# Carrying the scan state into the first source element on ScalarE instead of through the scan's initial value

## The chip, the cores and the metric

The kernel runs on one core of one Trainium2 chip. The metric is device time in microseconds (us) from the first to the last instruction of the program, as each run reports it; less is better. A profile is one further execution of the same program, recorded instruction by instruction. TensorE does matrix products, VectorE and GpSimd do elementwise work, ScalarE does activations and copies, and SyncE issues the transfers. In the profile's lines they are called PE, DVE, POOL, ACT and SP.

## The reference, cut to what matters

The reference is a network of four stages on an image batch of shape 4 x 96 x 64 x 64. Its first stage (`L0`) holds a selective scan, and that scan is most of the time. For each of 4 images and 4 directions (rows forward, columns forward, and both backward) the sequence has 4096 positions; there are 192 channels, and each channel has 16 states:

```python
def step(hst, inp):
    dt_t, x_t, B_t, C_t = inp
    dA = jnp.exp(dt_t[..., None] * A[None])
    dBx = dt_t[..., None] * B_t[:, :, None, :] * x_t[..., None]
    hst = hst * dA + dBx
    y_t = jnp.einsum('bkdn,bkn->bkd', hst, C_t)
    return (hst, y_t)
h0 = jnp.zeros((b, K, D_INNER, D_STATE), t.dtype)
```

So the state `hst` is a first-order recurrence along the sequence, multiplied by a decay `dA` and fed by a source `dBx` at each position. The rest of the network (a convolution, layer norms and an MLP, a second scan with one state per channel, an FFT stage, linear attention, two quantized MLPs) is work for each image that comes before or after its scan.

## The kernel before, in words

**Units.** A scan of one image and one direction is cut along the sequence into 4 chunks of 1024 positions (`CH`). The 192 x 16 = 3072 pairs of channel and state fill the 128 partitions 24 times. A *unit* is one such filling of one chunk: a tile of 128 x 1024. There are 4 images x 4 directions x 4 chunks x 24 = 1536 units, numbered `i`; unit `i` of chunk `s` (`s` = 0 to 3) continues unit `i - 24` of chunk `s - 1`. `steps[g]` gives image `b`, direction `k`, chunk number `s` and place `c`; for `k >= 2` the sequence runs backward, and the scan reads its tiles in reverse.

**What a unit does**, and on which engine:

- `sources()`, GpSimd: `w = u * bb`, the source (line `w<-u,bb` in the profile). `w` has 6 buffers.
- `decays()`, ScalarE: `h = Exp(dt * negA)`, the decay, into PSUM (`h<-dt,negA`). `h` has 2 buffers, so this `Exp` of unit `i` needs unit `i - 2` to be through.
- `recurs()`, VectorE: the scan, `h = scan(h, w)` (`h<-h,state,w` or `h<-h,w`), and then `w = h * cc` (`w<-h,cc`). In every 12th unit the scan writes `w` instead and GpSimd multiplies by `cc` (`side()`).
- `gathers()`, TensorE: four products with `sel4` sum `w` over the states into PSUM `py` (`py<-w,sel`), two units at a time.
- `decays()` again, two units later, ScalarE: where another chunk follows, a copy of the last column of `h` into `state[:, n]` (`state<-h`, 128 x 1).

In the kernel before, a scan in a chunk with `s > 0` has that column of `state` as its initial value, an operand of one number for each partition; in a chunk with `s = 0` its initial value is the constant 0.

**Order.** [...]each engine runs its instructions in the order in which they were issued. That order is made while the program is built by a planner, the class `Work`. The kernel is written as generators ("threads") that `yield on(engine, events...)` before each piece of work; the planner holds an estimated clock for each engine, picks the piece that can start first, and adds the estimated cost. `decays()` is its *lead* thread: `choose()` skips other ScalarE work that would hold up the lead. `latest()` tells by when the lead of a unit is due, out of the pace of the scans, with the constants `UNIT` (us a unit), `MARGIN` and `YIELD`; `AGE` lets ScalarE work that has waited long go ahead of the lead. All the work outside the scans (`others()`: fronts of later images, and for finished images `tail`, `l1`, `l2` and `back`) is background: it goes into the gaps beside the units. What is left of it when the last scan is over runs alone. For the last image `tail()` first normalizes four blocks of columns (`gate`, with its lines `yc<-...`), and then runs eight groups of 512 columns through a projection, a norm and an MLP (`group`, lines `x<-...`, `hn<-...`, `s<-...`), each ending in `stat<-x`; `l1` begins when all eight statistics are there.

Every VectorE and GpSimd instruction is recorded with line 254 (a helper), an activation with line 242, a ScalarE copy with line 231, a product with line 227. They are told apart by their tiles.

Of the kernel before, what the change touches and what calls it, by code (L numbers as in the profile page):

```python
# [12 lines left out]
AF = mybir.ActivationFunctionType  # L13
ALU = mybir.AluOpType
# [3 lines left out]
B, C, HH, WW = 4, 96, 64, 64  # L18
# [3 lines left out]
CH = 1024  # L22
# [3 lines left out]
UNITS = 24  # L26

LN_EXP = "natural_log_exp_and_others"
# [17 lines left out]
def size(x):  # L46
    return x.free_size() if hasattr(x, "free_size") else x[:].free_size()


def on(engine, *events, banks=0, took=0.7, table=None, unit=None):  # L50


    return engine, events, banks, took, table, unit
# [9 lines left out]
class Work:  # L63
# [2 lines left out]
    GAP = 0.25  # L66
    LEAD = 1.0
    PATIENCE = 0.0
    UNIT, MARGIN, YIELD, AGE = 3.6, 0.5, 0.8, 0

    def __init__(self):
        self.at = dict(pe=0.0, act=0.0, dve=0.0, pool=0.0, sp=0.0)
# [31 lines left out]
    def post(self, *key, stored=False):  # L104
        self.events[key] = self.me.stored if stored else self.me.end
# [111 lines left out]
def tile_hybrid(ctx: ExitStack, tc: tile.TileContext, I: dict, out: bass.AP):  # L217
    nc = tc.nc
    wk_ = Work()
# [9 lines left out]
    def copy(o, i, **kw):  # L229
        wk_.spend("act", 0.15 + size(o) * 0.87e-3)  # L230
        return nc.scalar.copy(o, i, **kw)  # L231

    def act(o, i, func, **kw):

        want = TABLES.get(func, func if func in OTHER else None)
        if want is not None and want != wk_.table:
            wk_.spend("act", 1.28)
            if func in TABLES:
                nc.scalar.preload_act_table_set(want)
            wk_.table = want  # L240
        wk_.spend("act", 0.2 + size(o) * 0.87e-3)
        return nc.scalar.activation(o, i, func, **kw)  # L242
# [25 lines left out]
    ve, po_ = Side(nc.vector, "dve", on_vector), Side(nc.gpsimd, "pool", on_pool)  # L268
# [27 lines left out]
    def open_banks(n, name="bk"):  # L296
        st, (p,) = pools(psum(name, 1))
        names = [f"{name}{k}" for k in range(n)]
        wk_.open(p, names)
        st.callback(wk_.close, names)  # L300
        return st
# [26 lines left out]
    def setup():  # L328
        yield on("act")
        act(negA, V("A", n=96), AF.Exp)  # L330
        act(l1A, V("l1A", n=2), AF.Exp)
        yield on("dve")
        ve.tensor_scalar_mul(negA, negA, -1.0)
        ve.tensor_scalar_mul(l1A, l1A, -1.0)
        for j in range(3):
            ve.reduce_sum(dsum[:, j : j + 1], V("Ds", j=4 * j, n=4), axis=mybir.AxisListType.X)
            ve.tensor_scalar(diagD[:, j], eye128, dsum[:, j : j + 1], None, ALU.mult)
        ve.reduce_sum(dsum[0:C, 3:4], V("l1D", C, n=2), axis=mybir.AxisListType.X)
        ve.tensor_scalar(centd, cent, dsum[0:C, 3:4], None, ALU.mult)
        for lay in (2, 3):  # L340
            yield from ffn_weights(lay)
# [986 lines left out]
    def rest(b):  # L1328
# [16 lines left out]
    steps = [  # L1345
        (b, k, s, NCH - 1 - s if k >= 2 else s) for b in range(B) for k in (0, 1, 3, 2) for s in range(NCH)
    ]
    NS_ = len(steps)
    NU = UNITS * NS_
    WB, DB, RB, SIDE = 6, 3, 5, 12  # L1350
    made, weights = {}, {}
    live = dict(h={}, w={}, state={}, Y=None, py=None)
    fg = {}

    def place(i):
        n = i % UNITS
        j, r = divmod(n, 8)
        q, p = divmod(r, 2)
        return i // UNITS, j, q, p, (2 * j + p) * 4 + q
# [104 lines left out]
    def decays():  # L1464
        for i in range(NU + 2):
            if i >= 2:
                yield on("act", ("scan" if (i - 2) % SIDE == SIDE - 1 else "C", i - 2), *([("dt", 6 * place(i)[0] + 2 * place(i)[1] + place(i)[3])] if i < NU else []), took=1.3, table=LN_EXP, unit=min(i, NU - 1))
                g, j, q, p, n = place(i - 2)
                b, k, s, c = steps[g]
                h = live["h"].pop(i - 2)  # L1470
                if s < NCH - 1:
                    last = 0 if k >= 2 else CH - 1
                    copy(live["state"][b, k][:, n : n + 1], h[:, last : last + 1])
                    post("st", i - 2)
            else:
                g, j, q, p, n = place(i)
                yield on("act", ("dt", 6 * g + 2 * j + p), took=1.3, table=LN_EXP, unit=i)
            if i < NU:
                g, j, q, p, n = place(i)
                k = steps[g][1]  # L1480
                h = live["h"][i] = fg["h"].tile([128, CH], F32, tag="h", name="h")
                act(h, made[g]["dt", 2 * j + p], AF.Exp, scale=negA[:, k * 24 + n : k * 24 + n + 1])
                post("h", i)

    def sources():
# [10 lines left out]
    def recurs():  # L1496
        for i in range(NU):
            g, j, q, p, n = place(i)
            b, k, s, c = steps[g]
            need = [("h", i), ("src", i), ("cc", 4 * g + q)]  # L1500
            if s:
                need.append(("st", i - UNITS))
            yield on("dve", *need)
            wk_.pace = i, max(wk_.me.start, wk_.at["dve"])
            if i % UNITS == 0 and s == 0:
                live["state"][b, k] = fg["ck"].tile([128, 24], F32, tag="state", name="state")
            h, w, state = live["h"][i], live["w"][i], live["state"][b, k]
            first = 0.0 if s == 0 else state[:, n : n + 1]
            o = w if i % SIDE == SIDE - 1 else h
            if k >= 2:  # L1510
                ve.tensor_tensor_scan(o[:, ::-1], h[:, ::-1], w[:, ::-1], first, ALU.mult, ALU.add)
            else:
                ve.tensor_tensor_scan(o, h, w, first, ALU.mult, ALU.add)
            if o is w:
                post("scan", i)
                live["h"][i] = o
                continue
            yield on("dve")
            ve.tensor_mul(w, h, made[g]["cc", q])
            post("C", i)  # L1520
# [99 lines left out]
    with tc.manual_schedule():  # L1620
        stb = open_banks(3, "bm")
        st = open_banks(5, "bs")
        mode["wide"] = True
        first = wk_.add(setup()), wk_.add(front(0))
# [10 lines left out]
        wk_.events["go",] = wk_.events["inproj", 0]  # L1635
        ts = [wk_.add(f(), 0) for f in (preludes, collects, convolved, gathers, side, sources)]
        wk_.lead = wk_.add(decays(), 0)
        ts += [wk_.lead, wk_.add(recurs(), 2), wk_.add(loads_du(), 0), wk_.add(loads_bc(), 0)]
        others_ = wk_.add(others())
        wk_.run(lambda: all(t.done for t in ts))  # L1640
# [181 lines left out]
```

## Time and profile before

| what | value |
|---|---|
| three runs, median (lowest to highest) | 6655.88 us (6654.35 to 6673.25) |
| the profiled execution's own time | 6648.81 us |
| its span, first to last instruction | 6647.0 us |
| mean granted TensorE clock | 0.871 |
| VectorE busy | 5807.2 us (87%) |
| GpSimd busy | 4740.5 us (71%) |
| ScalarE busy | 4308.0 us (65%) |
| TensorE busy (matmul) | 5289.4 us (80%) |

By stage, from the table of busy times in windows of the span:

| window, us | what runs | VectorE | ScalarE | GpSimd |
|---|---|---|---|---|
| 0 to 160 | front of image 0, first units | 39% | 42% | 27% |
| 700 to 6000 | units, with background beside them | 90 to 96% | 58 to 79% | 78 to 82% |
| 6085 to 6647 | rest of the last image, no units | 36% | 53% | 0% |

A group line of the profile reads: line, engine, operation, written tile `<-` read tiles, shapes, `x`count, then busy us and the mean ns of one, then how long the engine was idle just before these instructions and what ended that idle time. A line of the waits reads: who waited `<-` for whom, us in total, times, longest. A line of the timeline reads: start us, duration us, engine, line, operation, tiles.

### The profile page before, as it was taken

The numbers are of one execution on the slowest core, as the hardware profiler recorded it, in microseconds if no ns is written. First come the engines' busy times: TensorE is split into PE (matmuls) and PEld (weight loads), VectorE is DVE, ScalarE is ACT, GpSimd is POOL, SyncE is SP. The second block draws the span as 40 slices with busy tenths as digits, with TensorE's granted clock in tenths as the row PEclk, the third lists the DMA queues.
The fourth block names the chain that finished last, engine by engine and source line by source line (L and its number), as shares of the span: only waits on it lengthen the run. The fifth ranks groups of instructions, "written<-read, shape, count | busy, mean of one in ns | idle before, by whom it ended". The sixth has DMA issues, their size and how long they took to land. (4 is left out here: it accounts for less than half of the span.)

```text
span 6647.0 us, 55955 instructions
## 1 busy us (share of the span) xinstructions
PE 5289.4 (80%) x15752; PEld 1653.6 (25%) x15752; DVE 5807.2 (87%) x3872; ACT 4308.0 (65%) x6520; POOL 4740.5 (71%) x2148
## 2 busy tenths in 40 slices
PE   7678888977867888767777888877777888877788
PEld 2122221222211332212211232212211232212273
DVE  4898989899989999999989999999989999996613
ACT  4565756666766557876666567887666567885636
POOL 2778787787798787787698687787698687883000
PEclk8689999978879999888778999889778999888778
DMA  5656566565555685555555585555565586552451
GB/s 146 191 169 193 164 187 189 166 196 182 174 181 163 214 283 174 168 188 177 161 183 163 186 295 186 165 185 186 164 183 163 182 294 186 169 178 76 154 158 34
DMA packets 532384, 1189.24 MB, mean 179 GB/s; under 512 B 90158, under 2 KB 163451, under 8 KB 532060
## 3 DMA queue, kind: packets, MB, share of 16 engines
q1 hardware_dynamic: 532072, 1185.66, 57.0%
q8 instruction: 125, 2.05, 0.1%
q14 instruction: 187, 1.53, 0.1%
HBM read 937.80 MB, written 247.63 MB: 178 GB/s over the span
## 5 line engine op out<-in xcount | busy, mean ns | idle before, releaser
L254 POOL TENSOR_TENSOR w<-u,bb 128x1024 f32<-128x1024 f32 x1536 | 3607.6, 2374 | 907.0 <-PE py L227 785.3
L254 DVE TENSOR_TENSOR_SCAN h<-h,state,w 128x1024 f32<-128x1024 f32 x1056 | 2480.8, 2349 | 177.5 <-ACT h L242 89.2
L227 PE MATMUL py<-w,sel 128*32 128x512 f32 x6144 | 1847.9, 930 | 511.3 <-DVE w L254 381.7
L242 ACT ACTIVATE h<-dt,negA 128x1024 f32<-128x1024 f32 x1536 | 1727.7, 1125 | 428.5 <-DVE w L254 304.1
L254 DVE TENSOR_TENSOR w<-h,cc 128x1024 f32<-128x1024 f32 x1408 | 1721.8, 1223 | 109.5 <-DVE h L254 3.2
L254 DVE TENSOR_TENSOR_SCAN h<-h,w 128x1024 f32<-128x1024 f32 x352 | 805.5, 2288 | 112.7 <-POOL w L254 60.0
L231 ACT COPY state<-h 128x1 f32<-128x1 f32 x1056 | 166.2, 157 | 762.7 <-DVE w L254 761.1
L227 PEld LDWEIGHTS py<-w,sel 128*32 128x32 f32 x6144 | 188.0, 114 | 1595.7 <-DVE w L254 962.2
L254 POOL TENSOR_TENSOR w<-w,cc 128x1024 f32<-128x1024 f32 x128 | 301.9, 2358 | 165.6 <-ACT state L231 92.9
L227 PE MATMUL bm<-xp,dg 128*128 128x512 f32 x792 | 372.1, 616 | 0.9 <-ACT dtu L242 0.9
L227 PE MATMUL bm<-xi,xw 128*128 128x512 f32 x384 | 225.3, 733 | 99.8 <-DMA xi<-xi_d 84.6
L254 POOL TENSOR_TENSOR dtu<-dtu 128x1536 f32<-128x1536 f32 x64 | 221.3, 3458 | 84.7 <-ACT dtu L242 49.7
L242 ACT ACTIVATE dtu<-bm 128x512 f32<-128x512 f32 x384 | 209.0, 599 | 65.5 <-PE bm L227 62.8
L227 PE MATMUL bm<-xd,dtw 64*128 64x512 f32 x384 | 218.8, 654 | 21.8 <-ACT xd L242 9.9
L254 DVE TENSOR_TENSOR_SCAN w<-h,state,w 128x1024 f32<-128x1024 f32 x96 | 224.8, 2342 | 2.9 <-ACT h L242 2.7
L254 POOL TENSOR_TENSOR dtu<-dtu,xi 128x1536 f32<-128x1536 f32 x64 | 220.9, 3452 | 3.9
L227 PEld LDWEIGHTS bm<-xp,dg 128*128 128x128 f32 x792 | 148.5, 195 | 281.8 <-issue 263.0
L227 PE MATMUL bm<-big,dg 96*96 96x512 f32 x432 | 208.6, 625 | 10.8 <-ACT u L242 7.6
L227 PE MATMUL py<-Y,eye 128*128 128x512 f32 x288 | 166.2, 660 | 42.6 <-ACT Y L231 39.8
L242 ACT ACTIVATE bm<-bm,eps 96x512 f32<-96x512 f32 (+1 forms) x210 | 135.7, 646 | 64.7 <-PE bm L227 64.4
L242 ACT ACT_TABLE_LOAD x119 | 152.7, 1283 | 20.7 <-PE bm L227 18.7
L227 PE MATMUL bm<-x,cent 96*96 96x512 f32 x278 | 148.9, 628 | 19.6 <-DMA x<-in_x 5.5
(317 smaller groups left out, 6994.6 us busy)
## 6 DMA issues: line engine op xcount, KB each, us to landing
u<-dd SPq DMA_DIRECT2D x384, 512.0 KB
dt<-dd SPq DMA_DIRECT2D x384, 512.0 KB
bb<-bc SPq DMA_DIRECT2D x256, 512.0 KB
cc<-bc SPq DMA_DIRECT2D x256, 512.0 KB
dd<-dtu SPq DMA_DIRECT2D x256, 384.0 KB
xi<-xi_d SPq DMA_DIRECT2D x256, 192.0 KB
f_d<-fo SPq DMA_DIRECT2D x64, 384.0 KB
a<-f_d SPq DMA_DIRECT2D x64, 384.0 KB
```

The lines of the kernel that those rows point to most:

```text
L227: return nc.tensor.matmul(o, lhsT=lhsT, rhs=rhs, **kw)
L231: return nc.scalar.copy(o, i, **kw)
L242: return nc.scalar.activation(o, i, func, **kw)
L254: return f(o, *a, **kw)
```

## The change

The scan has the constant 0 as initial value in every unit. The carried state enters through the source: in units of chunks with `s > 0`, right after the `Exp` of the unit, ScalarE computes `w[:, e] = h[:, e] * state + w[:, e]` for the one column `e` at which the scan begins (the last for `k >= 2`, else the first). That is an Identity activation of 128 x 1 whose scale and bias are operands of one number for each partition. Since the scan's first output is `h[e] * initial + w[e]`, the result is the same. The add reads `w`, so ScalarE now needs GpSimd's product of the unit; the scan needs ScalarE's add. The scan's own event on the copied state is gone. Four planner numbers change with it: `UNIT`, `MARGIN`, `AGE` and the estimated cost (`took`) of the lead's piece.

```diff
-    UNIT, MARGIN, YIELD, AGE = 3.6, 0.5, 0.8, 0
+    UNIT, MARGIN, YIELD, AGE = 3.5, 1.0, 0.8, 0.3
...
     def decays():
...
-                yield on("act", ("scan" if (i - 2) % SIDE == SIDE - 1 else "C", i - 2), *([("dt", 6 * place(i)[0] + 2 * place(i)[1] + place(i)[3])] if i < NU else []), took=1.3, table=LN_EXP, unit=min(i, NU - 1))
+                yield on("act", ("scan" if (i - 2) % SIDE == SIDE - 1 else "C", i - 2), *([("dt", 6 * place(i)[0] + 2 * place(i)[1] + place(i)[3])] if i < NU else []), took=1.5, table=LN_EXP, unit=min(i, NU - 1))
...
                 act(h, made[g]["dt", 2 * j + p], AF.Exp, scale=negA[:, k * 24 + n : k * 24 + n + 1])
+                b, k, s, c = steps[g]
+                if s:
+
+                    if ("src", i) not in wk_.events:
+                        yield on("act", ("src", i), took=0.3, unit=i)
+                    e = slice(CH - 1, CH) if k >= 2 else slice(0, 1)
+                    w = live["w"][i]
+                    act(w[:, e], h[:, e], AF.Identity, scale=live["state"][b, k][:, n : n + 1], bias=w[:, e])
                 post("h", i)
...
     def recurs():
-            need = [("h", i), ("src", i), ("cc", 4 * g + q)]
-            if s:
-                need.append(("st", i - UNITS))
-            yield on("dve", *need)
+            yield on("dve", ("h", i), ("src", i), ("cc", 4 * g + q))
...
-            h, w, state = live["h"][i], live["w"][i], live["state"][b, k]
-            first = 0.0 if s == 0 else state[:, n : n + 1]
+            h, w = live["h"][i], live["w"][i]
             o = w if i % SIDE == SIDE - 1 else h
             if k >= 2:
-                ve.tensor_tensor_scan(o[:, ::-1], h[:, ::-1], w[:, ::-1], first, ALU.mult, ALU.add)
+                ve.tensor_tensor_scan(o[:, ::-1], h[:, ::-1], w[:, ::-1], 0.0, ALU.mult, ALU.add)
             else:
-                ve.tensor_tensor_scan(o, h, w, first, ALU.mult, ALU.add)
+                ve.tensor_tensor_scan(o, h, w, 0.0, ALU.mult, ALU.add)
```

## The prediction

> **What bounds the kernel now.** I read the page's row by slices first: VectorE is the fullest engine from the second slice to slice 36, and only then falls.
>
> ```profile
> DVE  4898989899989999999989999999989999996613
> ACT  4565756666766557876666567887666567885636
> ```
>
> Next, the groups of VectorE, and the waits.
>
> ```profile
> L254 DVE TENSOR_TENSOR_SCAN h<-h,state,w 128x1024 f32<-128x1024 f32 x1056 | 2480.8, 2349 | 177.5 <-ACT h L242 89.2 <-ACT state L231 54.3 <-POOL w L254 31.6
> L254 DVE TENSOR_TENSOR w<-h,cc 128x1024 f32<-128x1024 f32 x1408 | 1721.8, 1223 | 109.5 <-DVE h L254 3.2 <-PE bm L227 0.9 <-issue 0.3
> L254 DVE TENSOR_TENSOR_SCAN h<-h,w 128x1024 f32<-128x1024 f32 x352 | 805.5, 2288 | 112.7 <-POOL w L254 60.0 <-ACT h L242 30.0 <-ACT state L231 22.6
> L254 DVE TENSOR_TENSOR_SCAN w<-h,state,w 128x1024 f32<-128x1024 f32 x96 | 224.8, 2342 | 2.9 <-ACT h L242 2.7
> ...
> L254 DVE TENSOR_TENSOR_SCAN w<-h,w 128x1024 f32<-128x1024 f32 x32 | 72.9, 2279 | 0.0
> L254 DVE TENSOR_TENSOR_SCAN a<-bm,hp,a 96x512 f32<-96x512 f32 x46 | 58.0, 1262 | 3.1 <-POOL a L254 3.0
> ...
> L254 DVE TENSOR_TENSOR_SCAN a<-bm,a 96x512 f32<-96x512 f32 x6 | 7.2, 1196 | 0.0
> ```
>
> ```profile
> DVE h L254 <- ACT h L242: 119.2, 101, 14.8
> DVE h L254 <- POOL w L254: 91.6, 38, 44.3
> DVE h L254 <- ACT state L231: 76.9, 41, 12.2
> ```
>
> The reader is to see a natural experiment: the same tile with the state as operand takes 2349 ns, with the constant 2288, and so in the other pairs (2342 and 2279; in the second stage's shorter scan 1262 and 1196). The difference is 61 to 66 ns at either length, so it belongs to the instruction, not to the elements. VectorE pays it on its own time: in the timeline a unit is a scan and a product, back to back.
>
> ```profile
> 2301.96 2.35 DVE L254 TENSOR_TENSOR_SCAN h<-h,state,w 128x1024 f32<-128x1024 f32 x1
> 2304.42 1.23 DVE L254 TENSOR_TENSOR w<-h,cc 128x1024 f32<-128x1024 f32 x1
> 2305.56 2.35 DVE L254 TENSOR_TENSOR_SCAN h<-h,state,w 128x1024 f32<-128x1024 f32 x1
> ```
>
> The pitch is 3.60 us; the median over neighbouring units is 3.596 with the state and 3.533 with the constant. What VectorE waits for in the units is ScalarE (119 + 77 us) and GpSimd (92 us, 44 of it once, at the first unit). The last scan starts at 6079 us; behind it 562 us run without units, on other limits.
>
> **What the Trainium skill says.** "VectorE: DVE Perf Modes", Scalar operands: a scalar operand is a constant in the instruction or one number read for each partition. It gives no price for the second; this trace does, 61 ns. "ScalarE: Activation LUTs", Table sets: Identity is in every set, so I expect no table load with the add. "Perfetto Trace Analysis", Optimizing Scalar/DVE Operations: when VectorE is saturated, moving work to ScalarE may pay, but small instructions carry a fixed overhead. The trace agrees on the overhead (the 128x1 copy of the state takes 157 ns) and on the room: ScalarE is 58 to 79% busy beside the units.
>
> **The change part by part**, against the profiled execution (6648.8 us, span 6647.0; the median of the runs is 7.1 us above it).
>
> *1. Shorter scans.* 1056 x 61 ns + 96 x 63 ns = **-70.5 us**, all on VectorE's own path between the first and the last unit. It is lost where VectorE would only wait longer for ScalarE; that is in part 3.
>
> *2. The adds.* 1152 on ScalarE. The nearest row is an Identity with both operands per partition, `yc<-yc,vec` 128x512, 800 ns; taking off 511 elements at 0.88 ns (the `Exp` 1125 ns at 1024 elements and `x<-bm,vec` 675 at 512, both with one such operand) leaves 350 ns; it reads SBUF, and rows that read PSUM are 47 ns shorter (`xi<-xi,vec` 722, `x<-bm,vec` 675), so **0.30 us**. The bounds are 0.20 (`gm<-gm` 96x1, no such operand, 203 ns) and 0.37, the estimate from the price on the ScalarE page (186 ns and 93 for each operand). The add reads what the `Exp` has just written, so it starts after that has ended: dependent pairs in the trace start 0.03 us after the end, free ones 0.06 before. In all 1152 x (0.30 + 0.09) = some 450 us of ScalarE's queue, busy 346, hence from 65 to about 70%. Its idle time hides it, except that the scan is released 0.33 us later after its `Exp`. For most units this is covered: the median scan starts 2.09 us after the end of its `Exp`.
>
> *3. Waits on ScalarE.* Pairing each scan with its `Exp` in the timeline, 183 of the 1152 units start within 0.3 us of it: these were waiting, and get up to 183 x 0.33 = **+60 us**. Behind a waiting add stand, on ScalarE, the background, then the copy and the `Exp` of the next unit; TensorE waits for the background's evictions, and nothing on VectorE's unit path does. The add also waits for GpSimd: in 112 of these units `w` ended after the `Exp`, by 217 us in all. VectorE was mostly waiting there anyhow or was a unit behind, so I put 0 to +30 us on it, and take 0. Against this stands the new plan. I laid the background's ScalarE work, in the order of each program and with the durations of the trace, between consecutive `Exp`s: over 3 us there are 234 before and 208 after, over 5 us 34 and 17. Units with over 3 us hold 110 of the 200 us that ScalarE holds VectorE up. The excess over 4.8 us in two neighbouring units falls from 372 to 281 us, 25%; a quarter of 200 us is **-50 us** (bounds 0 and -80). Together **+10 us**.
>
> *4. The end.* Both programs hold the same background, but in the new order more of it comes after the last scan. The background runs behind: image 2's `back` reaches its copy `pa` after 1452 `Exp`s before, after 1479 now. Between the last gather and the statistics' product TensorE has 40 products before and 101 after; VectorE has 345 and 358 instructions after the last scan, ScalarE 531 and 586 after its last `Exp`. What leaves VectorE's unit path is some **-12 us** (three steps of `yc` at 1.75, six of `hn` and four of `stat` at 0.68, by these rows). What it costs at the end: 61 products of 0.86 us (`PE be` x20 in 8.60: two records each) are 52 us if TensorE is full. Between 6085 and 6147 us it was busy for 43 of 62 us, so up to 19 of them fill idle time. I take two thirds of that as filled: **+40 us** (33 to 60).
>
> *5. What is left.* The scan no longer waits for the copy from 24 units back: 0 us. That copy was over some 22 units, 80 us, before; the waits named `ACT state` are the end of ScalarE's latest instruction. No transfer is added (SP has 3566 instructions in both orders), and GpSimd's instructions are the same, with its background at slightly other places.
>
> Sum: -70.5 + 10 - 12 + 40 = -32.5 us, so 6616 against 6648.8, and **6623 us** against the median of 6655.9. The parts with the widest bounds are 3 and 4; both can take the gain of 1 or double it.
>
> **The rivals.**
>
> *Slower: the longer hand-over decides.* All 60 us of part 3 come, the add's wait for GpSimd costs its 30, the plan saves nothing and the end costs 60: -70.5 - 12 + 90 + 60 = +67.5, or 6723 us; 6698 with half of the plan's savings. Place: the scan's wait for `ACT w`. It decides from the point where waits and end add over 82 us. For it speak the 183 scans that follow their `Exp` at once; against it, the longest stretches of background get fewer.
>
> *No change.* Waits (+30) and end (+52) take the 82 us of parts 1 and 4: 6656. The gain is then to be seen in the units and lost behind the last scan.
>
> *A larger gain.* The plan's savings are 80 us and outweigh the hand-over: -70.5 - 12 + 60 - 80 + 35 = -67.5, or 6588 us; with the add at 0.20 us 18 us less.
>
> *The change does not do what it says.* Scans with a constant might stay at 2.35 us where they now follow the add. The 32 + 352 scans with the constant speak against it, in both directions of reading. It would give 10 - 12 + 40 = +38 us, or 6694; I count it to the slower case.
>
> **How the numbers follow.** 0.3% is 20 us, about what a measurement of this kernel can tell from no change: faster is below 6636, slower above 6676. The forecast (10 to 55 us less) has 0.46, of which 0.40 lies below 6636; the larger gain has 0.14, no change 0.17, slower 0.23. That makes faster 0.54, within 0.3% 0.23 and slower 0.23. The range leaves out the ends of both outer cases, a tenth each: 6570 to 6695.
>
> **What would show each step.** Part 1: all 1536 scans in rows `h<-h,w` and `w<-h,w` at 2.28 to 2.29 us, and a pitch of 3.53. Part 2: a row `w<-h,w,state` x1152 near 300 ns, no table loads beside it, ScalarE near 70%. Part 3: waits of `DVE h` for ScalarE in all, 196 us now, near 210 still; were they over 280, the slower case is right, and under 150 the larger gain. Part 4: the last scan starts near 6007 us (6079 - 70.5 + 10 - 12) and what follows takes some 608 us instead of 568. If the last scan starts later than 6060, the forecast is wrong.

## The result, and the profile after

The changed kernel takes 6682.93 us (median of 12 runs, 6669.8 to 6690.77) against 6662.93 us for the kernel before beside it (12 runs, 6646.92 to 6675.29). The ratio is **1.0029** (95% interval 1.0018 to 1.004): slower by about 20 us. The forecast was 6623.

The two profiled executions lie further apart, 6686.8 against 6647.0 us of span, since the one of before lies below its runs' median and the one of after above its own. I use them to see where the time went, and the ratios of the timed runs for how much it was.

The page's row by slices: VectorE is as full as before up to slice 36, and slice 37 falls to 3 where it was 6; ScalarE is up by a digit in many slices (4681.7 us busy, 70%, where it was 65%).

```profile
DVE  4899989899889999999889989999999989993613
ACT  4576767677866668887776667887876567885636
```

The groups (busy us and mean ns, then idle time ahead of them and what ended it). All 1536 scans now have the constant and last 2280 to 2289 ns in the mean, as announced. The add is the second line, 352 ns.

```profile
L254 DVE TENSOR_TENSOR_SCAN h<-h,w 128x1024 f32<-128x1024 f32 x1408 | 3223.2, 2289 | 337.9 <-ACT w L242 199.8 <-ACT h L242 81.3 <-ACT state L231 31.6
L242 ACT ACTIVATE w<-h,w,state 128x1 f32<-128x1 f32 x1152 | 405.1, 352 | 206.6 <-POOL w L254 103.5 <-ACT h L242 3.7
L254 DVE TENSOR_TENSOR_SCAN w<-h,w 128x1024 f32<-128x1024 f32 x128 | 291.9, 2280 | 10.7 <-ACT w L242 8.8 <-ACT state L231 1.3 <-ACT h L242 0.5
```

The waits (total us, times, longest). Those of the scans for ScalarE were 196 us and are now 313; 44.5 of them are the first unit, which had GpSimd's name before, so 268 compare. The main one, `ACT w`, is the add.

```profile
DVE h L254 <- ACT w L242: 199.8, 171, 15.2
ACT w L242 <- POOL w L254: 103.5, 71, 6.5
DVE h L254 <- ACT h L242: 81.3, 25, 44.5
DVE h L254 <- ACT state L231: 31.6, 22, 5.7
DVE h L254 <- POOL w L254: 23.4, 11, 5.4
```

The timeline gives the other loss. The last scan starts only 14 us earlier than before (6079.3), and from there to the instruction that joins the last statistics (`mv<-stat`) it is 122 us instead of 65. Before, then after:

```profile
6079.30 2.35 DVE L254 TENSOR_TENSOR_SCAN w<-h,state,w 128x1024 f32<-128x1024 f32 x1 [0.42 <-ACT h L242]
...
6144.45 0.37 DVE L254 BATCH_NORM_AGGREGATE mv<-stat 96x2 f32<-96x48 f32 x1
```

```profile
6065.07 2.28 DVE L254 TENSOR_TENSOR_SCAN w<-h,w 128x1024 f32<-128x1024 f32 x1
...
6187.18 0.37 DVE L254 BATCH_NORM_AGGREGATE mv<-stat 96x2 f32<-96x48 f32 x1
```

The busy times of these two stretches, before and then after (window, its length, then PE, PEld, DVE, ACT and POOL busy with instructions, clock, DMA share, GB/s): TensorE is the fullest engine in both, 74% and 85%.

```profile
6079.00:6144.00 65.00, 48.42 (x100) 16.64 (x96) 11.32 (x10) 29.97 (x38) 2.87 (x5) 0.87 0.15 43
```

```profile
6065.00:6187.00 122.00, 104.04 (x220) 37.30 (x218) 23.61 (x24) 69.28 (x90) 2.94 (x5) 0.92 0.16 43
```

To make one sum of it I added up VectorE's records in the timeline from the first scan to the last, each from its start to the start of the next less the idle time, and the idle time apart:

| us | before | after | difference |
|---|---|---|---|
| scans | 3554.4 | 3487.0 | -67.4 |
| products `w<-h,cc` | 1618.2 | 1622.5 | +4.3 |
| background on VectorE | 393.1 | 376.8 | -16.3 |
| idle | 380.2 | 445.5 | +65.3 |
| (of it ended by ScalarE) | 207.9 | 296.4 | +88.5 |
| last scan to `mv<-stat` | 65.2 | 122.1 | +56.9 |
| before the first scan, and after `mv<-stat` | 635.9 | 632.9 | -3.0 |
| span | 6647.0 | 6686.8 | +39.8 |

So the gain of part 1 is there in VectorE's busy time, its idle time has taken back as much, and the end costs 57 us.

### The profile page after: what moved, and what is told of

The parts are those of the page before. It is cut to its first block, busy times and chain, and to the rows that moved or that the text cites. A ratio compares the mean times of both kernels' runs of the same rounds, so it can differ in the third digit from the quotient of the medians.

```text
span 6686.8 us, 57304 instructions
## 1 busy us (share of the span) xinstructions
PE 5299.7 (79%) x15752; PEld 1668.0 (25%) x15752; DVE 5739.5 (86%) x3873; ACT 4681.7 (70%) x7680; POOL 4741.9 (71%) x2147
## 5 line engine op out<-in xcount | busy, mean ns | idle before, releaser
L254 DVE TENSOR_TENSOR_SCAN h<-h,w 128x1024 f32<-128x1024 f32 x1408 | 3223.2, 2289 | 337.9 <-ACT w L242 199.8
L227 PE MATMUL py<-w,sel 128*32 128x512 f32 x6144 | 1820.1, 948 | 542.6 <-DVE w L254 378.7
L242 ACT ACTIVATE w<-h,w,state 128x1 f32<-128x1 f32 x1152 | 405.1, 352 | 206.6 <-POOL w L254 103.5
L254 DVE TENSOR_TENSOR_SCAN w<-h,w 128x1024 f32<-128x1024 f32 x128 | 291.9, 2280 | 10.7 <-ACT w L242 8.8
L227 PE MATMUL bm<-big,dg 96*96 96x512 f32 x468 | 226.4, 627 | 4.1 <-ACT dt L242 1.6
L254 DVE TENSOR_TENSOR h<-h,bm 96x512 fp8e5<-96x512 f32 x52 | 34.4, 671 | 154.2 <-ACT bm L242 153.9
L242 ACT ACT_TABLE_LOAD x123 | 157.8, 1283 | 12.0 <-PE bm L227 9.6
```

Source lines behind the costliest of these rows:

```text
L227: return nc.tensor.matmul(o, lhsT=lhsT, rhs=rhs, **kw)
L254: return f(o, *a, **kw)
```

## The experiments

**The question.** Three things change at once: scans get shorter, ScalarE gets 1152 adds, and the planner lays out another order. Theories: the adds cost their hand-over (the scan released later), or their wait for GpSimd, or ScalarE's time; or the new order is what costs. All ratios are to the kernel before, run on the same chip; 0.001 is 6.7 us. A difference of two ratios is good to some 12 us (each ratio's interval is 5 to 11 us to either side), so I don't build on smaller ones.

### The change and the planner's numbers apart

`a_oldplan` is the changed kernel with the planner's old numbers; `b_newplan` is the kernel before with the new ones.

```diff
 a_oldplan, against after
-    UNIT, MARGIN, YIELD, AGE = 3.5, 1.0, 0.8, 0.3
+    UNIT, MARGIN, YIELD, AGE = 3.6, 0.5, 0.8, 0
...
-    took=1.5
+    took=1.3
```

> The changed kernel with the four planner numbers of the kernel before (UNIT 3.6, MARGIN 0.5, AGE 0, took 1.3). In its order 36 products are left between the last gather and the group statistics (40 in the kernel before, 101 in the changed one). Theory 1 (hand-over in the units, planner numbers at the end): the stretch from the last scan to the statistics goes back from 122 us to 60 to 70; scans stay 67 us shorter in all; ScalarE's holding up of VectorE in the units stays at 280 us or more (208 before, 296 changed), so the whole lands within 0.3% of the kernel before. Theory 2 (the planner numbers did all of the harm, in the units too): ScalarE's waits go back to about 210 us and the whole is 55 to 75 us faster than before.

> The kernel before, its scans with the state as initial value, with the four planner numbers of the changed kernel. 101 products are left behind the last gather. Theory 1: last scan to statistics about 120 us, waits on ScalarE in the units at or below the 208 us of before (160 to 210), the whole 20 to 50 us slower than before. Theory 2: waits on ScalarE near 290 us as in the changed kernel, the whole 110 us or more slower.

Measured: `a_oldplan` 6724.8 us, ratio 1.0092 (1.0077 to 1.0106); `b_newplan` 6695.37, 1.0053 (1.0041 to 1.0066). With the old numbers the end is the old one (62 us from the last scan to `mv<-stat`), and VectorE's idle time that ScalarE ends is 387 us (reckoned as in the table; so below too). With the new numbers and no adds the end is the new one (124 us), and that idle time is only 160. So the long end belongs to the numbers, not to the adds. The numbers cost 35 us without the adds and save 42 with them. The change itself, without its numbers, costs 61 us. It was expected within 0.3% of the kernel before; that the waits for ScalarE would rise to 387 us, far above the 296 of the changed kernel, was not foreseen.

### The order of the change without its adds, and with its adds for nothing

`a_noadd` keeps every instruction of the changed kernel in its order, but leaves out the adds, and with them the carried state. `a_ptr` keeps the adds and gives the scans their old initial value as well, so the state counts twice.

```diff
 a_noadd, against after
-                    act(w[:, e], h[:, e], AF.Identity, scale=..., bias=w[:, e])
+                    wk_.spend("act", 0.2 + 0.87e-3)
...
 a_ptr, against after
-                ve.tensor_tensor_scan(o, h, w, 0.0, ALU.mult, ALU.add)
+                ve.tensor_tensor_scan(o, h, w, first, ALU.mult, ALU.add)
```

> The changed kernel in its own order, with the 1152 adds left out (the planner still books their cost), so the carried state is left out of the computation. Theory 1: VectorE's waits on ScalarE in the units fall from 296 to about 210 us, the stretch behind the last scan stays at 115 to 125 us, the whole 65 to 90 us below the changed kernel, that is about 0.8% faster than before. Theory 2: without the adds the waits stay above 270 us, and the whole is within 20 us of the changed kernel.

> The changed kernel with its adds, but the scans take the state as initial value again (so the carried state is counted twice). It prices the shorter scan in the changed kernel's order. If the scans lie on the path that sets the end of the units: 60 to 70 us slower than the changed kernel (1.2 to 1.4% slower than before), with the waits on ScalarE unchanged. If the shorter scan was only exchanged for waiting (VectorE waits for ScalarE sooner): waits on ScalarE fall by 30 us or more and the whole is 40 us or less slower than the changed kernel.

Measured: `a_noadd` 6603.25, 0.991 (0.9896 to 0.9925); `a_ptr` 6712.03, 1.0068 (1.0055 to 1.0081). The adds cost 0.0119, or **79 us**, in the very order that was laid out for them. The shorter scans are worth 0.0039, 26 us, where their durations add up to 67: with the longer scans of `a_ptr` VectorE waits 58 us less for ScalarE (238 against 296). What the scans save is in large part waited away ahead of other scans.

### What of an add costs: ScalarE's time, the hand-over, or the wait for GpSimd

In the changed order, three steps. `a_load` puts at the add's place an activation that reads a column of `dt` (loaded long before) and writes a scratch tile nobody waits for: only ScalarE's time. `a_hand` lets it read `h`: it follows the `Exp`, and the scan, which overwrites `h`, has to wait for it: the hand-over too. The add itself also needs `w`: the wait for GpSimd. Neither scratch kernel carries the state.

```diff
-                    act(w[:, e], h[:, e], AF.Identity, scale=live["state"]..., bias=w[:, e])
 a_load
...
+                    act(live["scratch"][:, n : n + 1], x[:, e], AF.Identity, scale=live["state"]..., bias=x[:, e])
 a_hand
...
+                    act(live["scratch"][:, n : n + 1], h[:, e], AF.Identity, scale=live["state"]..., bias=x[:, e])
```

> The changed kernel in its own order, with each add turned into an activation of the same form that nothing waits for and that waits for nothing late: it reads one column of dt and writes a scratch column, so the carried state is left out of the result. It keeps ScalarE's time for the 1152 instructions (busy near 4690 us) and takes away both waits. The changed kernel is 79 us above the one without the adds. If the time on ScalarE is what costs: 50 us or more of these 79 stay (6650 us and more). If the delayed release of the scan costs: 0 to 25 us stay (6600 to 6630 us), and VectorE's waits on ScalarE are 150 to 175 us. If the add's wait for GpSimd's product costs: the same as for the release, so the next run has to tell these apart.

> As the run before, but the activation reads its column from h, so it starts after the Exp and the scan, which overwrites h, has to wait for it; it doesn't touch w, so it doesn't wait for GpSimd's product. The carried state is left out of the result. If the delayed release decides: within 25 us of the changed kernel (6660 to 6685 us), waits on ScalarE 250 us or more. If ScalarE standing in the add until GpSimd's product is there decides: 30 to 60 us below the changed kernel, close to the run without the release.

Measured: `a_load` 6633.41, 0.9961 (0.9948 to 0.9975); `a_hand` 6667.98, 1.0006 (0.9998 to 1.0014). From 0.991 the steps are +34 us for ScalarE's time, +30 for the hand-over, and +15 for GpSimd's product (to 1.0029). Each of the three alone is less than half of the 79. The 34 us lie between what was expected for the two cases (25 or less, 50 or more): neither theory holds alone. The idle time that ScalarE ends goes from 146 us (`a_noadd`) to 177, 221 and 296.

The same in the order of before, where no re-planning is mixed in. Four kernels take before's program and insert at the same 1106 units (in 46 of the 1152 the source isn't issued yet when ScalarE's turn comes, and they keep their operand): nothing (`b_in_none`, these units lose the state), the scratch activation on `dt` (`b_in_load`), the one on `h` (`b_in_hand`), and the real add (`b_inplace`). The planner books none of them.

```diff
 b_inplace, against before
                 act(h, made[g]["dt", 2 * j + p], AF.Exp, scale=...)
+                b, k, s, c = steps[g]
+                if s and i in live["w"]:
+                    e = slice(CH - 1, CH) if k >= 2 else slice(0, 1)
+                    w = live["w"][i]
+                    nc.scalar.activation(w[:, e], h[:, e], AF.Identity, scale=live["state"]..., bias=w[:, e])
+                    carried.add(i)
...
-            first = 0.0 if s == 0 else state[:, n : n + 1]
+            first = 0.0 if s == 0 or i in carried else state[:, n : n + 1]
```

> The kernel before in its own order to the last instruction on every engine, with the add put right behind the Exp of a unit and the scan's initial value 0 in 1106 of the 1152 units (in 46 GpSimd's product stands later in the program, and these keep the state). The planner books nothing, so nothing else is moved and 40 products stay at the end. Scans are 67 us shorter. If the adds cost what they cost in the changed kernel's order (80 us): 5 to 25 us slower than before, waits on ScalarE 280 to 310 us. If the order of before leaves the adds less room (as the changed kernel with the old planner numbers suggests: waits 387 us): 50 us or more slower, waits 340 us or more. If the 64 us of the prediction's sizing hold for an unmoved order: level with before.

> The order of before with the 1106 activations in the same places and the scans with the constant 0, but each activation reads a column of dt and writes a scratch column, so that no scan waits for it and it doesn't wait for GpSimd's product; the carried state is left out of the result. The adds cost 134 us in this order (69 us more in all, with 65 us shorter scans). If the split is as in the changed kernel's order (ScalarE's time 30, release 35, GpSimd 15): 6620 to 6640 us, 20 to 40 us below before. If in this order ScalarE's time is the larger part: 6650 us or more.

> As the run before, but the activation reads its column from h, so it follows the Exp and the scan waits for it; it still doesn't touch w. The carried state is left out of the result. The step from the run before is the price of the delayed release in the order of before, which the prediction put at up to 60 us (183 waiting scans x 0.33): 45 to 75 us if that count was right; under 40 us if a scan that waits had other reasons as well; over 80 us if the release delays more scans than those that waited.

> The order of before with the scans of the same 1106 units at the constant 0 and no activation in their place, so the carried state is left out there. It prices the shorter scan alone. If it lies wholly on the path: 1106 x 61 ns = 67 us below before (6585 to 6600 us). If VectorE turns part of it into waiting for ScalarE or GpSimd: 20 to 50 us below before, and the waits in the units grow by what is missing.

| kernel | median us | ratio (95%) | step |
|---|---|---|---|
| `b_in_none` | 6623.14 | 0.9947 (0.9933 to 0.996) | shorter scans: -35 us |
| `b_in_load` | 6681.9 | 1.0032 (1.002 to 1.0043) | ScalarE's time: +57 us |
| `b_in_hand` | 6718.52 | 1.0085 (1.0073 to 1.0097) | hand-over: +35 us |
| `b_inplace` | 6727.74 | 1.0098 (1.0084 to 1.0113) | GpSimd's product: +9 us, not told from none |

The waits of the scans for ScalarE and GpSimd between 140 and 6060 us, in `b_in_none`, then in `b_in_load`:

```profile
DVE h L254 <- ACT h L242: 133.3, 112, 14.9
DVE h L254 <- ACT state L231: 76.5, 41, 12.1
DVE h L254 <- POOL w L254: 54.0, 42, 2.6
```

```profile
DVE h L254 <- ACT h L242: 211.8, 196, 13.1
DVE h L254 <- POOL w L254: 79.8, 44, 12.5
DVE h L254 <- ACT state L231: 22.1, 12, 3.4
```

The scratch activation has no line of its own here: it releases no scan. `ACT h` and `ACT state` are best taken together, since the second only names ScalarE's latest instruction: 210 us in `b_in_none`, 234 in `b_in_load`. The waits for GpSimd's product make up the other half of the rise, 54 to 80 us. In the same window GpSimd's background (`x`) waits 71 us for ScalarE where it waited 37, so a part of ScalarE's time seems to reach the scan by way of GpSimd; no run separates that. In `b_in_hand`, and in `b_inplace`, the inserted instruction itself releases the scan:

```profile
DVE h L254 <- ACT scratch L1489: 166.7, 164, 5.9
```

```profile
DVE h L254 <- ACT w L1487: 231.1, 205, 11.8
...
ACT w L1487 <- POOL w L254: 49.6, 42, 2.9
```

How time on an engine that has idle time gets onto the path is to be seen in a stretch of the timeline of the changed kernel (start, duration, instruction; in brackets the idle time ahead of it and what ended it):

```profile
3004.36 0.35 ACT L242 ACTIVATE w<-h,w,state 128x1 f32<-128x1 f32 x1
3004.61 1.47 ACT L242 ACTIVATE dtu<-dtu 128x1536 f32<-128x1536 f32 x1
3006.11 1.57 ACT L242 ACTIVATE dtu<-dtu,one 128x1536 f32<-128x1536 f32 x1
3007.59 1.10 ACT L242 ACTIVATE h<-dt,negA 128x1024 f32<-128x1024 f32 x1
3008.78 0.35 ACT L242 ACTIVATE w<-h,w,state 128x1 f32<-128x1 f32 x1
...
3009.17 2.30 DVE L254 TENSOR_TENSOR_SCAN h<-h,w 128x1024 f32<-128x1024 f32 x1 [0.68 <-ACT w L242]
```

ScalarE runs back to back here. Behind one add stand two long background instructions, behind them the `Exp`, behind it the next add, and the scan starts 0.04 us after that. In such a stretch an add shifts what follows it. The 30% in which ScalarE is idle lies elsewhere, and work doesn't move there by itself: in the profile of before all 6281 activations and copies of ScalarE start in the order of the program (and so do the 3872 instructions of VectorE and the 2148 of GpSimd).

### Making the add free

If the hand-over is dear, the add can be taken out of it. `c_old` and `c_new` (old and new numbers) put the adds into a thread of their own, ahead of the unit's `Exp`: a small `Exp` of the one column for four units at a time gives the factor `he`, so that the add needs GpSimd but not the `Exp` of `h`.

```diff
+    def carries():
...
+            yield on("act", ("dt", ...), ("src", i), ("st", i - UNITS), took=0.4 if q else 0.7, table=LN_EXP, unit=i)
...
+                act(he, negA[:, k * 24 + n : k * 24 + n + 4], AF.Exp, scale=made[g]["dt", 2 * j + p][:, e])
...
+            act(w[:, e], live["he"][p][:, q : q + 1], AF.Identity, scale=live["state"]..., bias=w[:, e])
```

> The carried state is added to w without h: for each four units one Exp of 128x4 gives the decays of the first column out of negA and that column of dt, and the adds are a thread of their own, which the planner may place ahead of the unit's own Exp (748 of 1152 are). Planner numbers of the kernel before, so 36 products are left behind the last gather. If the delayed release is the main cost of the adds: waits on ScalarE 240 to 300 us where the changed kernel with these planner numbers has 387, the end at 60 to 70 us, the whole 20 to 60 us below that kernel's 6725 and, at best, 20 to 30 us below the kernel before. If the time on ScalarE or the wait for GpSimd is the main cost: waits on ScalarE stay above 350 us and the whole at 6700 us or more.

> As the run before with the planner numbers of the changed kernel: 84 products are left behind the last gather, so the end takes 100 to 115 us. If the delayed release is the main cost of the adds: waits on ScalarE 200 to 250 us (296 in the changed kernel), the whole 40 to 80 us below the changed kernel. If the time on ScalarE or the wait for GpSimd is the main cost: within 25 us of the changed kernel.

Both lost: `c_old` 6760.44, 1.0152 (1.0138 to 1.0166), and `c_new` 6728.86, 1.0104 (1.0088 to 1.012). `c_new` is 50 us above the changed kernel, where even the worse case expected had 25. The waits of ScalarE for GpSimd in `a_oldplan`, which has the same planner numbers, and in `c_old`:

```profile
ACT w L242 <- POOL w L254: 125.3, 74, 4.3
```

```profile
ACT w L242 <- POOL w L254: 203.1, 156, 4.1
```

Where the add stands ahead of the `Exp`, it waits longer for GpSimd, and the `Exp` stands behind it. Besides, 288 small `Exp`s of 287 ns take 83 us on ScalarE, and the add takes 381 ns there. These probably use up what the earlier release gives: VectorE's idle time that ScalarE ends is 383 us, and in `a_oldplan` 387. That the one has used up the other is argued, not shown. The 24 us by which the profile of `c_old` is the longer one aren't idle time at all; VectorE's background takes 22 us more (408 against 386), with 30 us more in one instruction, `a<-a,vec,cc`, that the last section shows.

`b_some400` and `b_some600` do the opposite: before's kernel and numbers, with the add only where the planner's clocks show 2.0 us (392 units) or 1.0 us (601 units) to spare; the others keep their operand.

```diff
 b_some400, against before
+                if s and src is not None and src + wk_.GAP <= now and now + 2.0 <= t0 + (i - i0) * wk_.UNIT:
...
+                    act(w[:, e], h[:, e], AF.Identity, scale=live["state"]..., bias=w[:, e])
+                    wk_.spend("act", 0.18)
+                    carried.add(i)
```

> The kernel before with its planner numbers, but a unit's state goes through the add on ScalarE (and its scan has the constant 0) only where the planner's clocks show GpSimd's product ready and 2.0 us to spare before the scan: 392 of 1152 units; the other 760 keep the state as initial value. Scans are 392 x 61 ns = 24 us shorter. If an add costs only where the scan is waiting for ScalarE or GpSimd is late: waits on ScalarE stay at 200 to 225 us and the whole is 8 to 24 us below before. If every add costs its share (80 us for 1152, 27 us for these): level with before or slower.

> As the run before with 1.0 us to spare: 601 of 1152 units add on ScalarE, scans 37 us shorter. If an add costs only where the scan is waiting: waits on ScalarE 210 to 240 us, the whole 10 to 35 us below before. If every add costs its share (42 us for these): level with before or slower, and slower than the run with 392.

Measured: `b_some400` 6710.45, 1.007 (1.0057 to 1.0083), and `b_some600` 6635.24, 0.9964 (0.9951 to 0.9976). Of the two cases expected, the first fits 601 adds and the second 392. More adds come out faster than fewer: that can't be the adds alone. So I took their orders without them: `b400_ptr` and `b600_ptr` issue what `b_some400` and `b_some600` issue, in the same order, with no add and every initial value as before. They do all the work of before in another order; the instructions are the same but for 10 and 12 more table loads on ScalarE (249 and 251, where before has 239).

```diff
 b400_ptr, against b_some400
-                    act(w[:, e], h[:, e], AF.Identity, scale=live["state"]..., bias=w[:, e])
+                    wk_.spend("act", 0.2 + 0.87e-3)
...
-                    carried.add(i)
```

> The order of the kernel with 601 adds, to the last instruction, without the adds: all scans of later chunks have the state as initial value. If the chosen adds pay by themselves: 10 to 35 us slower than the kernel with the adds (6645 to 6670 us). If the gain of that kernel came from the order that the planner happened to make: as fast as it or faster (6640 us or less).

> The order of the kernel with 392 adds without the adds, with the state as initial value. If its loss against before came from the order: within 25 us of 6710 us, or above it by up to 24 us. If the adds caused it: 6670 us or less.

Measured: `b600_ptr` 6637.17, 0.9964 (0.9952 to 0.9976); `b400_ptr` 6695.52, 1.0048 (1.0036 to 1.006). **The order alone moves this kernel by -24 and +32 us.** Within their orders, and with their shorter scans counted in, 601 adds cost nothing and gain nothing, and 392 adds cost some 15 us. The version that beats both kernels, by 24 us against before, owes nothing to the change.

### The numbers once more

`a_margin` has only `MARGIN` back at 0.5; `a_switch` has all four old numbers from unit 960 on. Both aim at the long end.

```diff
 a_margin, against after
-    UNIT, MARGIN, YIELD, AGE = 3.5, 1.0, 0.8, 0.3
+    UNIT, MARGIN, YIELD, AGE = 3.5, 0.5, 0.8, 0.3
...
 a_switch, against after
...
+            if i == 960:
+                wk_.UNIT, wk_.MARGIN, wk_.AGE = 3.6, 0.5, 0
```

> The changed kernel with MARGIN 0.5 as before, its other three planner numbers kept. 41 products are left behind the last gather (101 in the changed kernel). If the end and the units only trade with each other: last scan to statistics 60 to 70 us, waits on ScalarE in the units 340 us or more instead of 296, the whole within 20 us of the changed kernel (6665 to 6700 us). If MARGIN costs only at the end: waits stay near 296 us and the whole is 40 us or more below the changed kernel (below 6645 us).

> The changed kernel, whose planner numbers go back to those of the kernel before from unit 960 of 1536 on. 62 products are left behind the last gather. If the end and the units only trade with each other: last scan to statistics 80 to 90 us, waits on ScalarE 320 us or more, the whole within 20 us of the changed kernel. If the late units have room: waits 300 us or less and the whole 25 us or more below the changed kernel, level with the kernel before.

Measured: `a_margin` 6710.85, 1.0079 (1.0065 to 1.0093), and `a_switch` 6684.97, 1.0039 (1.0024 to 1.0054). `MARGIN` does set the end (41 products of TensorE behind the last gather, 62 us), but VectorE then waits 354 us for ScalarE instead of 296, and the whole is 33 us above the changed kernel, where at most 20 were expected; `a_switch` lies between (62 products, 77 us, 327 us). What the end gains the units lose, or more: background that isn't left for the end has to run beside the units.

### The account

In us, ratios by 6660. Shorter scans -35; ScalarE's time for the adds +57, hand-over +35, GpSimd +9, so **+66 in place** (1.0098). The new order with its numbers takes that to 1.0029, **-46**; in the profiles its end costs 54 us more than that of `b_inplace` (122 against 68), and from the first scan to the last it saves 90 (5932 us against 6021). Sum +20. These steps hold for this sequence of edits only: the same numbers cost 35 us where there are no adds, and the 46 units that `b_inplace` leaves out are in the last step.

## Why the prediction was wrong

**Part 1, shorter scans, -70.5.** The duration was right (-67.4 measured), its worth wasn't: -35 us in the order of before, -26 in the changed one (the two aren't told apart). A faster VectorE arrives earlier at the next `Exp`, and ScalarE isn't earlier: in `b_in_none` idle time grew by 26 us (380 to 406), 20 of it ended by ScalarE. The prediction had the sentence for this ("lost where VectorE would only wait longer for ScalarE"), sent it to part 3, and gave it no number there.

**Part 2, the adds: "Its idle time hides it". This is the step that failed most.** The add lasts 352 ns, not 300, inside the bounds and a small matter: the 47 ns taken off for reading PSUM came from rows of 128 and 96 partitions; with the same tile, `xi<-xi,vec` 722 and `xi<-bm,vec` 699, it is 23. The add brings no table load: `b_inplace` has 239 like before, and the eight more of the changed kernel (247, 1283 ns each) are in `b_newplan` too, which has no add. But the zero put for the time itself was +57 us in the order of before and +34 in the changed order. 1106 activations of 0.37 us are some 410 us of ScalarE's queue; a seventh of it came through. The cover that the prediction named was ScalarE's mean idle share, and the profile had already shown that this share doesn't cover every unit: VectorE's scans waited 196 us for an engine that was 65% busy. The skill's "Perfetto Trace Analysis", Optimizing Scalar/DVE Operations, says that offloading from a saturated VectorE may make sense; here the engine that takes the work is itself the one the saturated engine waits for, and in place the measurement decides against it.

**Part 3, the waits.** The release, put at +60, measured +35 and +30: right in kind, half in size. The wait for GpSimd, taken as 0 with 30 above, was +9 (not told from none) and +15. The new order's relief was put at -50 from the stretches of background between `Exp`s. That size was right: from `b_inplace` to the changed kernel the idle time that ScalarE ends falls from 348 to 296 us, and from before to `b_newplan`, both without adds, from 208 to 160. The rest of the 90 us saved in the units is other idle time, background that moved behind the last scan (16, part 4) and small things. Without the adds most of the relief was lost again, as the waits for GpSimd's product rose from 47 to 110 us. So the hand-over that the prediction took for the main risk was no larger than ScalarE's time in the changed order (30 against 34) and smaller in that of before (35 against 57). With -35 for part 1, +35 + 9 for the hand-over and GpSimd, and -46 for the order with its end, the sum would still have been a gain of 37 us; the term that turns it is ScalarE's time.

**Part 4, the end, +40 (33 to 60).** The mechanism was right: 61 more products on a TensorE that is 85% busy. They took 57 us, 0.93 each; letting a dozen us of them fill idle time was wrong, for TensorE's idle time in the stretch is 17 us before and 18 after. The -12 us of background moved behind the last scan were -16.

**The signs.** The last scan was to start at 6007 and the forecast was called wrong beyond 6060: it started at 6065. What follows was to take 608 us and takes 622. The scans' waits for ScalarE were to stay near 210, with over 280 for the slower case: 268 by the named waits, 296 by VectorE's idle time.

**The rivals.** The slower one had the sign, the place (`ACT w`) and the point, 82 us from waits and end, right: VectorE's idle time and the end together took 65 + 57. Its mechanism was half of it: hand-over and the wait for GpSimd are 44 of 101 us in the order of before and 45 of 79 in the changed one. ScalarE's time isn't in it, and the savings of the plan, which it put at nothing, came; that its sum points the right way is in part luck. The time lies inside the wide range (6570 to 6695) and outside the likeliest case.

**What stays open.** Why ScalarE's time costs 57 us in one order and 34 in the other isn't settled beyond the picture of full stretches; the two differ by little more than their uncertainty. No run separates which background instructions make the stretches full. The scratch activation that priced the time lasts 22 ns longer than the add, some 25 us over all of them, so a few us of that step may belong to the next.

## What to carry to other kernels

Work moved off the bounding engine isn't free on a less busy one if the bounding engine already waits for it: read who ends its waits, not the shares, and test the price with an instruction that costs the time and touches nothing. Where a planner lays out the order, put the edit into the old order before believing any sum, and measure the new order without the edit: here orders of the same work differ by up to 56 us, more than the edit's own net. A shorter instruction on a full engine is worth its saving only as far as its supplier keeps up; here it was half or less.

## What the runs showed of the hardware

The scratch activation takes 373 to 374 ns when it reads `dt` from SBUF (`b_in_load`, `a_load`) and 352 when it reads `h` from PSUM. The first is the estimate from the skill's "ScalarE: Activation LUTs", What ACT_TABLE_LOAD costs (186 ns and 93 for each of two operands, with 1 for the element: 373); for the second source the page has no figure.

One VectorE instruction of the second stage, `a<-a,vec,cc` on 96x512, takes 0.74 us in some of its 32 instances and up to 11 in others. In the timeline of `b_some400`, the instruction just before it takes 0.73, and the scan behind it starts eleven microseconds late; GpSimd meanwhile runs six products back to back, until 2008.43:

```profile
1997.16 0.73 DVE L254 SCALAR_TENSOR_TENSOR a<-dt,vec,bm 96x512 f32<-96x512 f32 x1
1997.93 11.05 DVE L254 SCALAR_TENSOR_TENSOR a<-a,vec,cc 96x512 f32<-96x512 f32 x1
2008.90 2.28 DVE L254 TENSOR_TENSOR_SCAN h<-h,w 128x1024 f32<-128x1024 f32 x1
```

```profile
1994.39 14.04 POOL L254 TENSOR_TENSOR w<-u,bb 128x1024 f32<-128x1024 f32 x6
```

The traces show what goes with it. Before, the 11 instances with no GpSimd instruction beside them take 0.74 to 0.75 us each; the 21 others take 0.98 to 7.98, with GpSimd at work for 93% of that time, and ten of these end 0.55 us after GpSimd has come to a pause. So it looks as if this instruction has to wait for a pause of GpSimd, and the wait is booked as busy time. It reads none of the tiles `w` that the six products write. Most other instructions of VectorE don't show it: `w<-h,cc`, which reads `h` from PSUM, takes 1.22 us with GpSimd beside it or without. That GpSimd is the cause wasn't tested by a run of its own.

Over the 32 instances it sums to 73.6 us before, 80.7 after, 95.7 in `b400_ptr` and 72.8 in `b600_ptr`, where 32 times 0.74 would be 24. So some 50 us of VectorE's busy time before go beyond the work of these instructions, more than the gain that was forecast: a busy share can hold waiting. Of what the order of `b400_ptr` costs (32 us by the timed runs, 47 in the profiles), 22 lie in this one instruction. In `b_inplace` and the three kernels of its series the sum is 72 to 76, so it doesn't touch those steps.
